# Mamba gate product in four parts beside the sums of its chunk pairs, its square in two, and a fourth tile of merged blocks in the last FFN

## The chip, the cores and the metric

The kernel runs on one core of one Trainium2 chip. Such a core has five engines that run at the same time, each taking its own instructions in their written order: TensorE (PE, matmuls; its weight loads are the row PEld), VectorE (DVE), ScalarE (ACT), GpSimd (POOL), and SyncE (SP), which here only issues DMAs. They meet through semaphores. The metric is the device time of one execution in microseconds (us), the median of several runs. PE reads the on-chip memory SBUF and writes PSUM[...].

## What is computed

The reference has two layers on an image batch of shape (4, 128, 64, 64). Layer 0 is a convolution-and-Mamba hybrid, layer 1 attention and a mixture-of-experts FFN. The change lies in layer 0. Its core is the Mamba block, cut to what matters:

```python
zxbcdt = x @ in_w.T + in_b
z, xBC, dt = ...                       # gate, conv input, step
xBC = _silu(conv3(xBC) + conv_b)       # xs, B, C
y = _ssd(xs * dt[..., None], dt * A, Bm, Cm)   # chunks of 64 tokens, states carried on
y = y + D[None, None, :, None] * xs
y = y.reshape(b, l, di) * _silu(z)             # the gate product
y = y * jax.lax.rsqrt(jnp.mean(y * y, -1, keepdims=True) + 1e-05) * rms_w
return y @ out_w.T
```

One Mamba runs on 8 seed channels made from the 128; two more, one after the other (a cascade), run on each of eight groups of 16 channels. Layer norms follow, and an FFN: a 1x1 convolution to 256 channels, a 3x3 depthwise convolution, GELU, a 1x1 convolution back. Everything is fp32.

## The kernel before, in words

**Items.** A picture has 4096 tokens; they are worked in blocks of 512, eight to a picture. One item is one Mamba on one block: 8 seed items and 4 batches x 8 blocks x 2 cascade levels = 64 cascade items, 72 in all. In a block there are `NU` = 4 pairs of 64-token chunks; `ng` is 2 for cascade items and 1 for seed items, so a tile such as `y` or `zs` holds 1024 or 512 elements in each of 128 partitions.

**Stages of an item.** `outer` loads and normalizes the block. `prep` makes the steps `dt`, their running sums `acs` (a DVE scan) and the decays; on POOL it makes `u` and `cdx`. `front` projects (PE: `ps_z`, `ps_x`, `ps_B`, `ps_C`; ACT: silu into `zs`, `xs`, `Bc`, `Cc`), forms the chunk products (`ps_g`, then `gm` on DVE) and the chunk states (`ps_st`), carries the states on by two DVE scans (`cd<-cd,ps_st`, with `inj` and a small add ahead of them), and multiplies the carried states with C (`ps_yo`, then `y<-ps_yo,y` on DVE). `back` forms the decay matrix (`ps_d`, then its exponentials `e` on ACT, weighed by `gm` on DVE: `e<-e,gm`), multiplies it with the inputs (`within(u)`: 64 matmuls into two PSUM banks, `bank<-e,xp`), and adds the sums to `y` for each chunk pair u: four DVE instructions `y<-bank,const,y`. When all four pairs are added, `back` goes on:

```python
nc.gpsimd.tensor_mul(zs, y, zs)            # L690
yield
yield
nc.scalar.activation(y, zs, AF.Square)     # L693
yield
...
pm = product("ps_ms", self.ms, by_token(y))   # L708
```

Then follow the logarithm and exponential for the root, the matmul `ps_out<-zs`, and the rest of the layer.

**What sets the order.** At a time `back` of one item, `front` of the next, `prep` of the one after and `outer` of a further one are recorded together, and, beside them, the FFN of the batch that was finished last. `Deck` records each instruction with the tiles it reads and writes; `flush` then lets a model of the engines choose the order on each. An instruction's rank is its place in the recording, moved by a table (`BEHIND`); a tile of a ring opens only when the ring has room; and the model never lets a POOL instruction and a DVE instruction with two SBUF inputs run at once (`lockers`, L934). The instructions are then issued in the order chosen, which the chip follows on each engine; so a change of one instruction's size or of its inputs can move others too. All instructions issued this way carry line 1031 in the profile, and are told apart by their tiles.

**FFN of layer 0.** `ffn` (L1348) goes over the eight blocks of a batch: `merge(k)` loads a block (`outs`), takes its layer norm and adds the seed part (`gf`, `ps_det`) and the normalized input (`xg`); `expand(k-1)` makes the 256 channels (`ps_h`, and `ps_hh` for the rows that border on the next block); `conv` does the depthwise taps on DVE (`acc`); `close(k-2)` applies the GELU, multiplies back (`ps_f`), adds on DVE (`t`) and POOL (`t<-t,xin`) and stores. The tiles `outs` have 3 buffers, `xg` (input blocks, used by `merge` and by `close`) 4, `acc` 3. The FFNs of the first three batches run beside the Mamba items; the last one runs when these are done, with four of nine taps on PE (`ps_taps`) and beside the first projections of layer 1 (`tk`, `xl`, `qf`, `kf`, `vf`).

Of the kernel before, what the change touches and what calls it, by code (L numbers as in the profile page):

```python
# [20 lines left out]
F32 = mybir.dt.float32  # L21
F32R = mybir.dt.float32r
U32 = mybir.dt.uint32
AF = mybir.ActivationFunctionType
# [7 lines left out]
LB = 512  # L32
# [243 lines left out]
class Mamba:  # L276
# [344 lines left out]
    def back(self, it, out):  # L621
        sh, s, nc = self.sh, self.s, self.sh.nc
        work, const, ng = sh.work, sh.const, s.ng
        y, zs = it["y"], it["zs"]
        y4 = y.rearrange("p (u g c l) -> p u g c l", u=NU, g=ng, c=2)
        es = {}

        def exponentials(u):
            rt = it["rt"]
            ds = [sh.wide("ps_d") for _ in range(2)]  # L630
            for j2 in range(2):
                for g in range(ng):
                    for j in (2 * j2, 2 * j2 + 1):
                        rows = slice(32 * j, 32 * j + 32)
                        dv = ds[j2][:, j % 2, 0:256 * ng].rearrange("s (h g l) -> s h g l", h=4, g=ng)
                        for c in range(2):
                            nc.tensor.matmul(dv[:, :, g, :], lhsT=sh.lt[rows, g, u, Q * c:Q * c + 128],
                                             rhs=rt[rows, :, u, c, :], start=c == 0, stop=c == 1)
            es[u] = []
            for k in range(2):  # L640
                e = work.tile([128, 4, 2, ng * Q], F32, tag="e", bufs=E_BUFS, name="e")
                nc.scalar.activation(e.rearrange("s h j x -> s j h x"),
                                     ds[k][:, :, 0:256 * ng].rearrange("s j (h x) -> s j h x", h=4), AF.Exp)
                es[u].append(e)

        def weigh(u):
            U, i = divmod(u, 2)
            for k, e in enumerate(es[u]):

                e2 = e.rearrange("s h j x -> s h (j x)")  # L650
                gm = it["gm"][U][:, 2 * i + k].rearrange("s j x -> s (j x)")
                nc.vector.scalar_tensor_tensor(e2, e2, 1.0, gm[:, None, :].to_broadcast([128, 4, 2 * ng * Q]),
                                               ALU.min, ALU.mult)

        def within(u):
            U, i = divmod(u, 2)

            pyv = [t[:, 0:128 * ng].rearrange("p (h x) -> p h x", h=2) for t in sh.psy.tiles("py")]
            for k, e in enumerate(es.pop(u)):
                for g in range(ng):  # L660
                    for f in range(2):
                        for jj in range(2):
                            j = 2 * k + jj
                            for c in range(2):
                                rows = slice(64 * c, 64 * c + 64)
                                nc.tensor.matmul(pyv[c][32 * j:32 * j + 32, :, Q * g:Q * g + Q],
                                                 lhsT=it["xp"][U][rows, g, 4 * i + j, 16 * f:16 * f + 32],
                                                 rhs=e[rows, 2 * f:2 * f + 2, jj, Q * g:Q * g + Q],
                                                 start=f == 0, stop=f == 1)
            for f, name in enumerate(("even", "odd")):  # L670
                for c in range(2):
                    part = pyv[c][:, f, :].rearrange("p (g l) -> p g l", g=ng)
                    nc.vector.scalar_tensor_tensor(y4[:, u, :, c, :], part, const(name), y4[:, u, :, c, :],
                                                   ALU.mult, ALU.add)

        exponentials(0)
        yield
        exponentials(1)
        weigh(0)
        yield  # L680
        for u in range(NU):
            within(u)
            if u + 1 < NU:
                weigh(u + 1)
            if u + 2 < NU:
                exponentials(u + 2)
            yield


        nc.gpsimd.tensor_mul(zs, y, zs)  # L690
        yield
        yield
        nc.scalar.activation(y, zs, AF.Square)  # L693
        yield

        def by_token(t):
            return t.rearrange("p (u g c l) -> p g c u l", u=NU, g=ng, c=2)

        def product(name, lhsT, rhs):

            p, n = sh.ps(name), 128 // ng
            for g in range(ng):
                rows = slice(n * g, n * g + n)
                nc.tensor.matmul(p[rows].rearrange("p (c u l) -> p c u l", c=2, l=Q), lhsT=lhsT[:, g, rows],
                                 rhs=rhs[:, g], start=True, stop=True)
            return p

        pm = product("ps_ms", self.ms, by_token(y))  # L708
        r = y[:, 0:LB]
        nc.scalar.activation(r, pm, AF.Ln, bias=sh.eps, scale=4.0 / s.nh)  # L710
        yield
        nc.scalar.activation(r, r, AF.Exp, scale=-0.5)
        yield
        yield
        out(product("ps_out", self.wo, by_token(zs)), r)
        yield
# [428 lines left out]
def layer0(tc, T, td, const, ident, eps, where, batches, qkv):  # L1145
# [8 lines left out]
    nc = tc.nc  # L1154
    with ExitStack() as ctx:
# [47 lines left out]
        deck = Deck(nc)  # L1203
        nc = sh.nc = deck
# [5 lines left out]
        work = ring(ctx, "work", 2)  # L1210
# [5 lines left out]
        sh.psy = Halves(deck, scan.enter_context(tc.tile_pool(name="psy", bufs=1, space=PSUM)))  # L1216
        gfd = dram.tile([128, L], F32, name="gfd")

        def load(b, k, work=work):
            xin = work.tile([128, LB], F32, tag="xg", bufs=4, name="xin")  # L1220
            nc.sync.dma_start(out=xin, in_=T["x"][b, :, blk(k)])
            return xin

# [124 lines left out]
        def ffn(b, work, ps, depth=0, diag=0, taps=None, ps_taps=None):  # L1348
# [18 lines left out]
            def merge(k):  # L1367

                y = work.tile([128, LB], F32, tag="outs", bufs=3 + depth, name="outs")
                outs[k] = y  # L1370
                nc.sync.dma_start(out=y, in_=td[b, :, blk(k)])
                yield
                yield
                pm = ps("ps_mean")
                nc.tensor.matmul(pm, lhsT=const("avg"), rhs=y, start=True, stop=True)
                nc.vector.scalar_tensor_tensor(y, y, gmix, pm, ALU.add, ALU.subtract)
                yield
                r = work.tile([128, LB], F32, tag="sq", name="ln_r")
                nc.scalar.activation(r, y, AF.Square)
                gf = work.tile([128, LB], F32, tag="ys", name="gf8")[0:8, :]  # L1380
                nc.sync.dma_start(out=gf, in_=gfd[32 * b:32 * b + 8, blk(k)])
                xg = load(b, k, work)
                yield
                pv = ps("ps_var")
                nc.tensor.matmul(pv, lhsT=const("avg"), rhs=r, start=True, stop=True)
                rsqrt(nc, r, pv, eps)
                yield
                nc.vector.tensor_mul(y, y, r)
                normed(b, xg)
                pd = ps("ps_det")  # L1390
                nc.tensor.matmul(pd, lhsT=P("detok", slice(0, 8)), rhs=gf, start=True, stop=True)
                nc.vector.scalar_tensor_tensor(y, y, P("n2w"), pd, ALU.mult, ALU.add)
                nc.vector.scalar_tensor_tensor(y, y, bias2, xg, ALU.add, ALU.add)
                yield
# [38 lines left out]
            def conv(k):  # L1433

                accs[k] = []
                for g in range(2):
                    acc = work.tile([128, LB], F32, tag="acc", bufs=3 + depth, name="acc")
                    sums = made[k].pop(0) if k in made else None
                    for i in range(diag, 9):
                        w = P("dw")[:, 9 * g + i:9 * g + i + 1]  # L1440
                        if sums is None:
                            nc.vector.tensor_scalar(rows(acc), tap(g, i), w, None, ALU.mult)
                        else:
                            nc.vector.scalar_tensor_tensor(rows(acc), tap(g, i), w, sums, ALU.mult, ALU.add)
                        sums = rows(acc)
                        if i % 3 == 2:
                            yield
                    accs[k].append(acc)

            def close(k):  # L1450
# [2 lines left out]
                for g, a in enumerate(acc):  # L1453
                    nc.scalar.activation(a, a, AF.Gelu_apprx_tanh, bias=P("dw_b")[:, g:g + 1])
                nc.scalar.preload_act_table_set(LNEXP)
                xin = load(b, k, work)
                yield
                pf = ps("ps_f")
                for g in range(2):
# [69 lines left out]
        def single(tag, bufs):  # L1529
            return lambda name: pp.tile([128, LB], F32, tag=tag, bufs=bufs, name=name)  # L1530

        pending = deck.staged("ffn", ffn(pending, last, single("f", 4), 0, 4, taps, single("t", 2)))
        run((pending, FFN), (deck.staged("early", early()), 5 * NBLK + 7))
        deck.flush(tc)

# [501 lines left out]
```

## Time and profile before

| | |
|---|---|
| median of 3 runs | 8414.19 us (8400.1 to 8424.57) |
| profiled execution | 8410.01 us |
| its span, first to last instruction | 8408.0 us |
| granted PE clock, mean | 0.948 |
| Mamba items, with the first three FFNs | 60 to 3540 us |
| last item's end, last FFN with first projections | 3540 to about 3763 us |
| attention and experts | from there to the end |

The page of the profile gives busy times of each engine and the costliest groups of instructions. A group is named by line, engine, operation and tiles, written as output<-inputs. The view of waits gives who waited for whom in total; the timeline gives single instructions with their start, length and the idle time ahead of them; stage windows give busy times in stretches of the span. All can be cut to a stretch, an engine or a tile.

### The profile page before, as it was taken

What the parts mean: (1) busy time and instruction counts of PE and PEld (TensorE: products, weight loads), DVE (VectorE), ACT (ScalarE), POOL (GpSimd) and SP (SyncE); (2) the same over time, 40 slices, a digit from 0 to 9 for tenths busy, and PEclk for the clock granted to TensorE, in tenths of its full rate; (3) what the DMA queues carried; (4) which work ended last, traced back from release to release, by engine and by line L of the source; (5) the groups of instructions that cost most, each with busy time, mean ns of one, the idle gap of its engine ahead of it and who ended that gap; (6) DMA issues with size and microseconds to landing.
All of it is one profiled execution on the core that took longest, in us unless ns stands there. A gap on an engine that the chain in (4) does not pass through costs nothing.

```text
span 8408.0 us, 191225 instructions
## 1 busy us (share of the span) xinstructions
PE 7635.6 (91%) x80284; PEld 4548.2 (54%) x80284; DVE 6326.8 (75%) x11211; ACT 5095.5 (61%) x6444; POOL 4737.9 (56%) x3225
## 2 busy tenths in 40 slices
PE   5888888888888888789999999999999999999998
PEld 3566666666666666534554555555555545555554
DVE  6767667887788788767777777777777777777775
ACT  5767677777777777654555555555555555555554
POOL 1111111111111111107999999999999999999997
PEclk8899899988999999889999999999999999999999
DMA  4211111121121112135454545454545545444442
GB/s 143 84 51 45 54 47 50 54 56 50 51 58 52 51 54 57 34 122 132 125 133 125 130 118 138 120 127 128 127 122 132 131 120 131 118 119 119 120 120 60
DMA packets 306604, 800.54 MB, mean 95 GB/s; under 512 B 43984, under 2 KB 61008, under 8 KB 288848
## 3 DMA queue, kind: packets, MB, share of 16 engines
q1 hardware_dynamic: 304848, 780.94, 35.3%
q8 instruction: 633, 10.37, 0.5%
q10 hardware_dynamic: 432, 5.12, 0.2%
q0 software_dynamic: 464, 2.25, 0.1%
q14 instruction: 227, 1.86, 0.1%
HBM read 595.19 MB, written 192.94 MB: 94 GB/s over the span
## 4 chain that ended last, share of the span: by engine, by line
PE 51%; POOL 25%; DVE 10%; ACT 7%; issue 5%; DMA 2%; SPq 0%; POOLq 0%; DVEq 0%; ACTq 0%
POOL s L1885 14%; PE ps_mx L1841 7%; POOL es L1887 6%; PE acc L1900 6%; PE ps_s L1879 5%; PE bank L1031 4%; PE ps_s L1873 3%; PE ps_x L1031 2%; PE ps_B L1031 2%; PE ps_d L1031 2%; DVE y L1031 2%; PE ps_C L1031 2%; PE ps_yo L1031 2%; DVE e L1031 2%; POOL zs L1031 1%
## 5 line engine op out<-in xcount | busy, mean ns | idle before, releaser
L1843 DVE TENSOR_REDUCE mx<-ps_mx 128x1 f32<-128x512 f32 x4096 | 2789.4, 688 | 818.8 <-PE ps_mx L1841 811.4
L1883 ACT ACTIVATE e<-ps_s 128x1024 f32<-128x1024 f32 x2048 | 1985.9, 1022 | 1723.9 <-PE ps_s L1879 1604.5
L1885 POOL TENSOR_TENSOR s<-e 128x1024 f32<-128x1024 f32 x1024 | 2442.8, 2386 | 210.4 <-ACT e L1883 205.0
L1841 PE MATMUL ps_mx<-k,q 128*128 128x512 f32 x4096 | 1879.3, 468 | 57.4 <-DVE mx L1843 23.2
L1887 POOL TENSOR_TENSOR es<-s 128x512 f32<-128x512 f32 x1024 | 1312.1, 1281 | 80.3
L1879 PE MATMUL ps_s<-q,k 128*128 128x512 f32 x4096 | 1281.7, 394 | 0.0
L1900 PE MATMUL acc<-e,V 128*32 128x512 f32 x8192 | 1096.3, 607 | 0.0
L1841 PEld LDWEIGHTS ps_mx<-k,q 128*128 128x128 f32 x4096 | 774.9, 189 | 528.7 <-DVE mx L1843 216.9
L1879 PEld LDWEIGHTS ps_s<-q,k 128*128 128x128 f32 x4096 | 773.3, 189 | 138.6 <-issue 2.7
L1031 DVE SCALAR_TENSOR_TENSOR e<-e,gm 128x1024 f32<-128x1024 f32 (+1 forms) x576 | 663.3, 1162 | 28.8 <-ACT e L1031 27.3
L1873 PEld LDWEIGHTS ps_s<-mr,ones 32*128 32x128 f32 x4096 | 200.4, 181 | 889.9 <-ACT e L1883 414.7
L1031 ACT ACTIVATE e<-ps_d 128x1024 f32<-128x1024 f32 (+1 forms) x576 | 547.0, 974 | 111.3 <-PE ps_d L1031 92.1
L1031 POOL TENSOR_TENSOR u<-acs 128x512 f32<-128x512 f32 x72 | 74.8, 1039 | 926.5 <-DVE acs L1031 907.2
L1031 DVE SCALAR_TENSOR_TENSOR y<-bank,const,y 128x128 f32<-128x128 f32 (+1 forms) x1152 | 365.8, 336 | 266.1 <-PE bank L1031 264.2
L1873 PE MATMUL ps_s<-mr,ones 32*128 32x512 f32 x4096 | 531.5, 496 | 20.3 <-ACT e L1883 20.3
L1031 PE MATMUL bank<-e,xp 64*32 64x128 f32 x17408 | 473.3, 283 | 62.6 <-DVE y L1031 59.1
L1031 PE MATMUL ps_d<-rt,lt 32*128 32x256 f32 x4352 | 422.4, 317 | 52.1 <-ACT y L1031 15.1
L1031 PEld LDWEIGHTS bank<-e,xp 64*32 64x32 f32 x17408 | 373.1, 110 | 145.7 <-DVE y L1031 99.3
L1031 PEld LDWEIGHTS ps_d<-rt,lt 32*128 32x128 f32 x4352 | 306.4, 195 | 222.3 <-ACT e L1031 49.9
L1900 PEld LDWEIGHTS acc<-e,V 128*32 128x32 f32 x8192 | 161.4, 108 | 363.5 <-issue 356.0
L1031 PE MATMUL ps_ms<-y,const 128*64 128x512 f32 (+1 forms) x272 | 133.7, 1033 | 237.7 <-ACT y L1031 233.7
L1031 POOL TENSOR_TENSOR zs<-y,zs 128x1024 f32<-128x1024 f32 (+1 forms) x72 | 173.6, 2411 | 311.1 <-DVE y L1031 311.0
(349 smaller groups left out, 11961.3 us busy)
## 6 DMA issues: line engine op xcount, KB each, us to landing
k<-kd SPq DMA_DIRECT2D x512, 512.0 KB, 7.1
x<-hl SPq DMA_DIRECT2D x256, 256.0 KB, 5.1
V<-vd SPq DMA_DIRECT2D x128, 512.0 KB, 11.4
cd<-raw SPq DMA_DIRECT2D x256, 256.0 KB, 5.2
parts<-cd SPq DMA_DIRECT2D x128, 512.0 KB, 5.6
xin<-in_x SPq DMA_DIRECT2D x128, 256.0 KB, 3.6
q<-qd SPq DMA_DIRECT2D x512, 64.0 KB, 4.5
hl<-hi SPq DMA_DIRECT2D x72, 256.0 KB, 2.0
```

Of the source, the lines that this page charges most:

```text
L1031: getattr(getattr(self.nc, op.engine), name)(*[self.real(a) for a in args], **{k: self.real(a) for k, a in kw.items()})
L1841: nc.tensor.matmul(p, lhsT=q4s[u][:, 128 * qt:128 * qt + 128], rhs=k4s[u][:, blk(kb)], start=True, stop=True)
L1843: nc.vector.tensor_reduce(mxs[u][:, qt, kb:kb + 1], p, AX.X, ALU.max)
L1873: nc.tensor.matmul(pts[j // 2][:, j % 2, :], lhsT=ones2[rows, :], rhs=mrows[u][rows, :], start=True, stop=False)
L1879: nc.tensor.matmul(pts[j // 2][:, j % 2, :], lhsT=k4s[u][:, 128 * kt:128 * kt + 128], rhs=q4s[u], start=False, stop=True)
L1883: nc.scalar.activation(e[:, 2 * j:2 * j + 2], pts[j], AF.Exp)
L1885: nc.gpsimd.tensor_add(s2, e[:, 0:2], e[:, 2:4])
L1887: nc.gpsimd.tensor_add(s, s2[:, 0], s2[:, 1])
L1900: nc.tensor.matmul(accs[u][32 * j:32 * j + 32, :], lhsT=Vs[u][:, 4 * g + j, :], rhs=e[:, j, :], start=g == 0, stop=g == 7)
```

## The change

The gate product is issued in `back`'s loop over the chunk pairs, right after the work of pair u, and only on that quarter of the tile (256 elements for cascade items, 128 for seed items). The square is issued as two ACT instructions, one for each half. In the FFN, the parameter `depth` now adds to the buffers of `outs` and takes from those of `xg`, while `acc` stays at 3; the last FFN is called with depth 1 (4, 3, 3) in place of 0 (3, 4, 3). The other FFNs keep depth 0. The numbers of steps (`yield`) in `back` stay as they were.

```diff
             if u + 2 < NU:
                 exponentials(u + 2)
+
+            part = slice(256 * ng // 2 * u, 256 * ng // 2 * (u + 1))
+            nc.gpsimd.tensor_mul(zs[:, part], y[:, part], zs[:, part])
             yield
 
 
-        nc.gpsimd.tensor_mul(zs, y, zs)
-        yield
-        yield
-        nc.scalar.activation(y, zs, AF.Square)
+        yield
+        yield
+        half = 256 * ng
+        for part in (slice(0, half), slice(half, 2 * half)):
+            nc.scalar.activation(y[:, part], zs[:, part], AF.Square)
         yield
...
-        def load(b, k, work=work):
-            xin = work.tile([128, LB], F32, tag="xg", bufs=4, name="xin")
+        def load(b, k, work=work, bufs=4):
+            xin = work.tile([128, LB], F32, tag="xg", bufs=bufs, name="xin")
...
-                xg = load(b, k, work)
+                xg = load(b, k, work, 4 - depth)
...
-                    acc = work.tile([128, LB], F32, tag="acc", bufs=3 + depth, name="acc")
+                    acc = work.tile([128, LB], F32, tag="acc", bufs=3, name="acc")
...
-                xin = load(b, k, work)
+                xin = load(b, k, work, 4 - depth)
...
-        pending = deck.staged("ffn", ffn(pending, last, single("f", 4), 0, 4, taps, single("t", 2)))
+        pending = deck.staged("ffn", ffn(pending, last, single("f", 4), 1, 4, taps, single("t", 2)))
```

## The prediction

> **What bounds the kernel now.** The page comes first: TensorE (PE) is busy 91% of the span, no other engine over 75%. Cut by stage, the scan stage that the change touches lies at 60 to 3540 us. Columns: busy us of PE, weight loads, DVE, ACT, POOL, with instruction counts; then clock and DMA share.
>
> ```profile
> PE 7635.6 (91%) x80284; PEld 4548.2 (54%) x80284; DVE 6326.8 (75%) x11211; ACT 5095.5 (61%) x6444; POOL 4737.9 (56%) x3225
> 60.00:3540.00 3480.00, 2948.07 (x54190) 2121.41 (x54195) 2638.24 (x4490) 2508.12 (x3336) 447.06 (x537) 0.90 0.20 55
> ```
>
> PE is busy 2948 of 3480 us here, DVE 2638, ACT 2508, POOL 447. What matters is the 532 us that PE idles: the view of waits, cut to PE and this stretch (total us, times, longest).
>
> ```profile
> PE ps_ms L1031 <- ACT y L1031: 227.3, 59, 7.6
> PE bank L1031 <- DVE y L1031: 59.1, 89, 2.4
> PE ps_yo L1031 <- DVE cd L1031: 42.1, 27, 4.0
> ```
>
> One wait is 43% of it: `ps_ms`, the mean square over heads, waits for the square, which waits for the gate product. Now one item in the timeline, item 25 of 72 (start, length, engine; last bracket: idle before).
>
> ```profile
> 1217.87 1.56 PE L1031 MATMUL bank<-e,xp 64*32 64x128 f32 x62 [0.16 <-DVE y L1031]
> 1219.36 2.07 PE L1031 MATMUL ps_st<-xd,bT 64*64 64x32 f32 x128
> 1221.97 0.34 DVE L1031 SCALAR_TENSOR_TENSOR y<-bank,const,y 128x128 f32<-128x128 f32 x1
> 1222.78 2.35 POOL L1031 TENSOR_TENSOR zs<-y,zs 128x1024 f32<-128x1024 f32 x1
> 1225.17 1.06 ACT L1031 ACTIVATE y<-zs 128x1024 f32<-128x1024 f32 x1 [1.59 <-POOL zs L1031]
> 1226.28 1.98 PE L1031 MATMUL ps_ms<-y,const 128*64 128x512 f32 x4 [4.85 <-ACT y L1031]
> 1226.44 1.22 DVE L1031 TENSOR_TENSOR_SCAN cd<-cd,ps_st 128x512 f32<-128x512 f32 x1
> 1229.02 0.65 PE L1031 MATMUL ps_yo<-Cc,last_casc 64*32 64x64 f32 x16
> ```
>
> The last sum `y` ends at 1222.31. Product and square follow (POOL's `u` holds the product back by 0.47), and `ps_ms` starts 3.97 us after `y`, PE having idled 4.85. Over the 63 full cascade items the chain from `y` to `ps_ms` averages 3.92 us: start 0.26, product 2.51, square 1.06, handovers 0.09. But DVE is busy throughout: its second state scan `cd`, which `ps_yo` needs, ends only at 1227.66. That sets how much of the wait can be gained.
>
> [...]
>
> ```profile
> 1479.13 2.81 POOL L1031 TENSOR_TENSOR zs<-y,zs 128x1024 f32<-128x1024 f32 x1
> 1479.66 2.84 DVE L1031 TENSOR_TENSOR sd<-sd,u 128x512 f32<-128x512 f32 x1
> ```
>
> The gate product first waits for DVE's two-input `a`, then runs its 2.35 us while `sd`, 0.68 us when alone, waits for it and takes 2.84. [...]
>
> **The change part by part.**
> *Product.* One POOL instruction becomes four. 1024 elements take 2.35 us and 512 (seed items, shortest) 1.28: a slope of 2.09 ns per element, so 256 take 0.75. The 160-wide `cdx` (0.53 us) lies on the same line. Only the last part follows the last `y`: 2.51 becomes 0.75 on the chain. POOL's total grows from 2.35 to 3.0 us an item, which its 13% load hides.
> *Square.* 1024 elements cost 1.06 us, 512 cost 0.63 (both rows exist). The first half can run early; the chain keeps 0.63. ACT pays 0.2 us more an item, hidden in its 28% idle; without that cover 13 us. The written order holds two more table loads (1.28 us each): 3 us at most.
> *Chain.* 0.3 start + 0.75 + 0.63 + 0.1 = 1.8 us against 3.92: 2.1 us less. Over the items that wait this would be about 125 us.
> *What is late next.* After `ps_ms`, PE needs `ps_yo`, hence the second `cd`. I walked the written order of both kernels over 62 cascade items with durations from the rows. PE's work from the last `bank` to `ps_ms` (mean 3.3 us before, 3.4 after) starts 3.86 us ahead of the last `y`'s end (measured; 3.64 in the changed order, where DVE has 0.22 us less between the pair's sums). `ps_ms` may not start before the chain ends, nor `ps_yo` past its first 16 matmuls before DVE has worked from the last `y` to the second `cd` (5.0 us before, 4.9 after). The walk gives for before 250 us waiting at `ps_ms` and 36 at `ps_yo`, 286 together, against 227 and 42 measured, so it reads about 6% high. For the changed order it gives 116 and 97: 213. The chain gains 134, the scan takes 61 back; net 73 us. In some items the changed order even puts `ps_yo` ahead of `ps_ms`; these gain least.
> *Seed items.* Parts of 128 elements (0.48 us) and half squares (0.41) cut a 2.4 us chain to 1.05, eight times; but the order moves a `ps_g` out of the cover (1.1 us): 5 us net.
> *Port.* Three parts an item now fall between DVE's two-input `e<-e,gm`. If half the parts meet one and hold it 0.35 us, that is 0.5 us of DVE an item, 40% of it reaching PE: 13 us. The last part sometimes meets `inj` or `a`: 0.1 us an item, 6 more. Cost 20. Bounds: -15 (before's own collisions, like the 2.84 above, vanish) to +142 (3 x 0.75 x 63, all on the path).
> *Last FFN.* `outs` gets a fourth buffer, the `xg` ring falls from four to three; `acc` stays three, and the middle FFNs keep their sizes.
>
> ```profile
> 3673.12 0.74 DVE L1031 SCALAR_TENSOR_TENSOR t<-ps_f,pb,outs 128x512 f32<-128x512 f32 x1
> 3673.89 0.32 SPq L1031 DMA_DIRECT2D outs<-td  x1
> 3676.59 1.12 PE L1031 MATMUL ps_mean<-outs,const_sb 128*128 128x512 f32 x2 [0.19 <-DMA outs<-td]
> ```
>
> The load is issued 0.03 us after `t` frees the buffer; with a fourth it need not wait. The `xg` load of a merge now takes the slot that the POOL add of three blocks before freed; that add ended a block ago, so SP, where the load stands ahead of the projections' stores, does not stop there. From 3590 to 3763 us PE idles 20 us, about 10 of it in this chain (waits of `ps_var` 6.8, `ps_mean` 1.6, `ps_h` 1.5). Bounds 0 to -10; I take -6.
> *Sum.* -73 - 5 + 20 - 6 = -64, against the profiled execution's own 8410 us (span 8408): 8346. The runs' median is 4 us higher, so 8350. Attention, from 3763 on, is untouched.
>
> **Rivals.**
> *The whole wait is gained.* DVE idles 24% of the scan, so its queue might follow PE forward. Against: item 25, where DVE never rests from `y` to `cd`. 125 + 5 + 6 less 10 for the port is 126: about 8288.
> *Everything is given back.* DVE's work between `y` and `cd` differs in the rewritten order from item to item (1.4 to 7.6 us); if `ps_yo` loses 1 us an item more than walked, 62 us go and the gain with them: about 8412.
> *Slower[...].* The early parts lie beside `e<-e,gm`, which feeds `bank`, PE's largest work. If every part stops DVE for its 0.75 us on that path, 142 us are lost against 84 gained: 8414 + 58 = 8472. It decides against the change when DVE loses over 1.3 us an item on the path. For it: `e` stands right behind the pair's sums in many items. Against: [...] 24% idle time.
>
> **How the numbers follow.** Half given back: 0.50, own range 8315 to 8387. Whole wait: 0.16, 8250 to 8315. Given back: 0.16, within 0.3% (25 us, about what a measurement here can tell). Slower: 0.18, 8439 to 8480, its middle near 8450, since not every part will stop DVE fully. Faster is the first two, 0.66. The range for eight in ten drops the far halves of the whole-wait and the slower case (0.17): 8280 to 8450.
>
> **What would show it.** Right: `zs` four times an item near 0.75 us; squares 0.63; `ps_ms <- ACT y` falls from 227 to near 120 while `ps_yo <- DVE cd` rises from 42 to near 95; the scan stage some 60 us shorter. Wrong: `ps_yo` unchanged (whole gain), or `e<-e,gm` well over its 1222 ns mean and more `bank` wait (port), or new waits elsewhere from the rewritten order, which the walk doesn't see beyond `ps_yo`; `outs` loads still issued right behind `t`.

## The result, and the profile after

The changed kernel takes 8399.12 us (median of 19 runs, 8375.46 to 8422.16) against 8414.19 (19 runs, 8400.1 to 8433.43): a ratio of 0.998, with a 95% interval of 0.9971 to 0.999. That is 15 us, a small gain, and less than the 25 us that the prediction called about what a measurement here can tell. The forecast was 8350. The time lies in its range, 8280 to 8450, but in the case that it called given back (chance 0.16), not in the likeliest one. One run of the study, of e2 below, took 10815 us at a mean clock of 0.606, far from all others, and is left out of e2's numbers.

The profiled execution took 8403.3 us against 8410.01. First the stage view of the kernel after, for the stretch of the scan (busy us of PE, weight loads, DVE, ACT, POOL; then the granted clock, DMA share and GB/s):

```profile
60.00:3540.00 3480.00, 2995.92 (x53841) 2143.47 (x53842) 2608.38 (x4471) 2504.73 (x3394) 607.60 (x748) 0.89 0.20 55
```

PE is busy 48 us longer than before in this stretch and has done less in it: 53,841 matmuls against 54,190. Now the view of waits for PE of the kernel after, in the same stretch (total us, times, longest):

```profile
PE ps_ms L1035 <- ACT y L1035: 115.7, 49, 4.8
PE ps_yo L1035 <- DVE cd L1035: 84.4, 49, 3.0
PE bank L1035 <- DVE y L1035: 35.3, 48, 2.1
...
PE ps_g L1035 <- DVE gm L1035: 30.5, 24, 2.4
```

The two waits that the forecast worked out came as told: 227.3 became 115.7 (forecast 116) and 42.1 became 84.4 (forecast 97), together 69 us less. And yet the last of the 72 items reaches its `ps_ms` at 3570.3 us, against 3551.9 before: the scan got 18 us *longer*. Up to that point PE idled 496 us in place of 538, which is 42 less; but it was busy 3015 us in place of 2954, 61 more, with the same 54,296 matmul records. The groups of instructions say how that can be. Kernel before, then after (last part: busy us, mean ns of one):

```profile
L1031 PE MATMUL ps_out<-zs,wc_casc 128*64 128x512 f32 x252 | 79.6, 715 | 0.4
L1031 PE MATMUL ps_ms<-y,const 128*64 128x512 f32 x252 | 118.7, 1040 | 216.1 <-ACT y L1031 216.1
```

```profile
L1035 PE MATMUL ps_out<-zs,wc_casc 128*64 128x512 f32 x252 | 102.9, 908 | 1.3 <-ACT ln_r L1035 0.5 <-ACT y L1035 0.4
L1035 PE MATMUL ps_ms<-y,const 128*64 128x512 f32 x252 | 108.0, 951 | 104.3 <-ACT y L1035 101.8 <-DVE cd L1035 2.6
```

The same 252 matmuls of `ps_out`, of the same shape, went from 715 to 908 ns: more of them ran at half clock. One item shows it, item 14 (counted from 0) in PE's timeline (start, length; last bracket: idle before). Before:

```profile
706.60 1.97 PE L1031 MATMUL ps_ms<-y,const 128*64 128x512 f32 x4 [4.05 <-ACT y L1031]
708.51 0.90 PE L1031 MATMUL ps_cd<-cdx,const 128*128 128x160 f32 x2
...
712.83 0.74 PE L1031 MATMUL ps_d<-rt,lt 32*128 32x256 f32 x8
713.50 1.08 PE L1031 MATMUL ps_out<-zs,wc_casc 128*64 128x512 f32 x4
```

After:

```profile
702.32 1.16 PE L1035 MATMUL ps_g<-Cc,Bc 64*64 64x64 f32 x64 [1.73 <-DVE gm L1035]
...
709.77 0.72 PE L1035 MATMUL ps_yo<-Cc,cd 64*32 64x64 f32 x32 [1.54 <-DVE cd L1035]
712.87 2.36 PE L1035 MATMUL ps_yo<-Cc,cd 64*32 64x64 f32 x80 [2.37 <-DVE cd L1035]
715.16 1.22 PE L1035 MATMUL ps_d<-rt,lt 32*128 32x256 f32 x8
716.31 1.98 PE L1035 MATMUL ps_ms<-y,const 128*64 128x512 f32 x4
...
720.20 1.98 PE L1035 MATMUL ps_out<-zs,wc_casc 128*64 128x512 f32 x4
```

Before there is one long wait, and the half clock that begins in it (705.87 to 712.69 us) is over after some 6 us of work: `ps_d` runs in 0.74 us and `ps_out` in 1.08. After, the written order has `ps_yo` ahead of `ps_ms`. There are three shorter waits (1.73, 1.54, 2.37), and the wait for the square is quite gone; but `ps_d` takes 1.22 and `ps_out` 1.98, as `ps_ms` does. The stage view of the kernel after gives the clock of these stretches (columns as above):

```profile
690.00:711.30 21.30, 16.38 (x540) 13.41 (x536) 17.51 (x30) 13.31 (x20) 6.27 (x6) 0.92 0.03 7
711.30:724.90 13.60, 12.03 (x115) 7.38 (x116) 7.17 (x9) 5.88 (x8) 2.13 (x2) 0.50 0.01 2
```

For 13.6 us the clock stood at half, with 12 us of work in it.

The trace records the granted clock over time; laid over PE's busy stretches it splits them into work at full and at half clock. The table does this from 60 us to the last item's first `ps_ms`. "Full-clock work" is busy time less half of the time at half clock, an estimate from these two of what the same work would take at full clock.

| kernel | last `ps_ms` at | PE idle | PE busy | of it at half clock | full-clock work |
|---|---|---|---|---|---|
| before | 3551.9 | 538 | 2954 | 554 | 2676 |
| after | 3570.3 | 496 | 3015 | 688 | 2671 |

The work is the same to 0.2%; in these two profiles the busy time differs because 134 us more of it ran at half. Half of that is 67 us, which covers the 61.

But a profile is a single run. The mean granted clock is on record for every run. The clock is 1.0 or 0.5 throughout the traces of before and after; where that holds, the missing share of the mean, doubled, times the span, is the time at half clock. The mean is 0.9448 over the 19 runs of after, and 0.9459 to 0.9473 over the sets of runs of before that the experiments were set against. The profiled run of before, at 0.948, lies above these means, that of after, at 0.944, below its own. By the means the change has some 15 to 40 us more time at half clock in the whole kernel, where the two profiles are 77 us apart. So the profiles show the direction and overstate the size.

### The profile page after: what moved, and what is told of

Same layout as the page of the kernel before. It is cut to its first block, busy times and chain, and to the rows that moved or that the text cites. A ratio compares the mean times of both kernels' runs of the same rounds, so it can differ in the third digit from the quotient of the medians.

```text
span 8401.5 us, 191443 instructions
## 1 busy us (share of the span) xinstructions
PE 7681.8 (91%) x80284; PEld 4579.0 (55%) x80284; DVE 6315.2 (75%) x11211; ACT 5105.5 (61%) x6518; POOL 4902.6 (58%) x3441
## 4 chain that ended last, share of the span: by engine, by line
PE 30%; POOL 21%; issue 3%; DVE 2%; ACT 1%; DMA 0%; SPq 0%; POOLq 0%; DVEq 0%; ACTq 0%
POOL s L1889 13%; PE ps_mx L1845 7%; PE acc L1904 6%; POOL es L1891 6%; PE ps_s L1883 6%; PE ps_s L1877 3%; PE ps_e L1793 2%; PE ps_den L1917 1%; DVE mx L1847 1%; PE ps_taps L1035 1%; PE ps_sh L1864 0%; POOL parts L1707 0%; PE ps_f L1782 0%; POOL cx L1709 0%; PE ps_f L1781 0%
## 5 line engine op out<-in xcount | busy, mean ns | idle before, releaser
L1035 POOL TENSOR_TENSOR zs<-y,zs 128x256 f32<-128x256 f32 (+1 forms) x288 | 314.1, 1091 | 1256.3 <-DVE y L1035 1255.6
L1800 DVE SCALAR_TENSOR_TENSOR acc<-ps_e,w,acc 128x128 f32<-128x128 f32 x896 | 312.5, 349 | 47.6 <-PE ps_e L1793 15.2
L1035 DVE SCALAR_TENSOR_TENSOR acc<-h,pb,acc 128x512 f32<-128x512 f32 x448 | 338.1, 770 | 7.8
```

The source lines that it names most:

```text
L1035: getattr(getattr(self.nc, op.engine), name)(*[self.real(a) for a in args], **{k: self.real(a) for k, a in kw.items()})
L1800: nc.vector.scalar_tensor_tensor(acc, pe[:, 128 * j:128 * j + 128], we, acc, ALU.mult, ALU.add)
```

## The experiments

Theory of the clock: the edit trades one long wait for more, shorter ones, and PE's clock stands at half for longer. Theory of the order: the edit is good, but the order that `Deck` newly plans for it costs as much as it gains. Theory of the port, by the prediction's name for it: the parts hold up VectorE, as the product did `sd` there (2.84 us, 0.68 when alone). What is behind this no run shows. The part in the last FFN is taken off first. Times are set against runs of the kernel before on the same chip; ratios are given with their 95% intervals.

**The last FFN alone (e1).** The kernel before with the FFN hunks of the diff only:

```diff
-            xin = work.tile([128, LB], F32, tag="xg", bufs=4, name="xin")
+            xin = work.tile([128, LB], F32, tag="xg", bufs=bufs, name="xin")
...
-        pending = deck.staged("ffn", ffn(pending, last, single("f", 4), 0, 4, taps, single("t", 2)))
+        pending = deck.staged("ffn", ffn(pending, last, single("f", 4), 1, 4, taps, single("t", 2)))
```

> The kernel before with the last FFN's part of the change alone (a fourth tile of merged blocks); the scan is untouched. The prediction had priced this part at -6 us. The two traces instead show the stretch from the last square's sum to the first sum of the attention going from 236.9 to 214.9 us. If that belongs to the FFN's part, this kernel takes 8392 us, 22 us less than before, with the scan's last sum at the same place (3552 us) as before. If it is the scan's changed end that gave it, the gain is near 6 us or below.

Measured: 8404.42 us, ratio 0.999 (0.9979 to 1.0): 13 us less, in an interval that reaches 1.0. From the last `ps_ms` to the first sum of the attention (`ps_mx`) its profile has 224.3 us against 236.9, also 13 less. So the FFN's part gives about 13 us, between the 22 and the 6 of the expectation. The waits of PE in the last FFN, 3597 to 3757 us of this run:

```profile
PE ps_mean L1031 <- DVE kf L1031: 9.1, 5, 2.0
PE ps_q L1031 <- ACT v L1031: 4.0, 1, 4.0
```

The waits on the chain of `outs` (`ps_var`, `ps_h`, and `ps_mean` for the load; 6.8, 1.5 and 1.6 us before) are gone; others grew, `ps_mean` for `kf` from 4.6 us and `ps_q` from 0.2.

**The scan's part alone (e2).** The changed kernel with the last line of the diff undone:

```diff
-        pending = deck.staged("ffn", ffn(pending, last, single("f", 4), 1, 4, taps, single("t", 2)))
+        pending = deck.staged("ffn", ffn(pending, last, single("f", 4), 0, 4, taps, single("t", 2)))
```

> The scan's part of the change alone (product in four, square in two); the last FFN as before. Every theory that adds the two parts up expects what e1 leaves: if e1 gains 22 us, this one is 5 to 18 us slower than before (8419 to 8432), with the scan's last sum near 3570 us against 3552, TensorE's idle time in the scan some 36 us lower and its busy time some 60 us higher. If e1 gains only 6 us, this one gains 9.

Measured: 8409.35 us (median of 13 runs), ratio 0.9989 (0.9977 to 1.0): 8 us less, nearer to the second case of the expectation than to the first. With e1's 13 us the two parts add up to some 20 us, the change's 15 to within what can be measured. In this kernel's profile the last `ps_ms` stands at 3575.4, PE idles 500 and is busy 3015 us, 685 of it at half clock. So the scan's part by itself is worth nothing that can be told from zero.

**The split in the old order (e3).** The planner sees the whole product and the whole square, and plans the order of before; the parts are issued as soon as the sums of their pair are:

```diff
+            for extra in list(self.extras):          # in flush, behind each issued op
+                extra[0].discard(id(op))
+                if not extra[0]:
+                    self.extras.remove(extra)
+                    for engine, name, args in extra[1]:
+                        getattr(getattr(self.nc, engine), name)(*[self.real(a) for a in args])
...
         nc.gpsimd.tensor_mul(zs, y, zs)
+        nc.ops[-1].calls = [("tensor_mul", (zs[:, part[3]], y[:, part[3]], zs[:, part[3]]), {})]
+        for u in range(3):
+            nc.extras.append((pair_done[u], [("gpsimd", "tensor_mul", (zs[:, part[u]], y[:, part[u]], zs[:, part[u]]))]
+                              + [("scalar", "activation", (y[:, half[0]], zs[:, half[0]], AF.Square))] * (u == 2)))
...
         nc.scalar.activation(y, zs, AF.Square)
+        nc.ops[-1].calls = [("activation", (y[:, half[1]], zs[:, half[1]], AF.Square), {})]
```

> The kernel before with its written order kept on every engine: parts 0 to 2 of the product are issued right behind the sums of their pair, the fourth part and the second half of the square stand where the whole ones stood, the first half right behind part 2. The last FFN as before. Theory of the clock (shorter and more frequent waits leave TensorE's granted clock at half for longer): the waits ahead of the sum fall as in the change, by 90 to 110 us, but TensorE's busy time in the scan rises by 30 to 60 us from 2954, and the time is 8340 to 8400. Theory of the order (the newly planned order of the scan costs the time, the split gains it): the walk over the old order with the parts in it gives 100 us less than before, busy time rises by at most 15 us, and the time is 8310 to 8340. Theory[...] (the parts hold up VectorE): no gain, 8400 to 8440, with VectorE's instructions beside the parts longer.

**The new order without the split (e4).** The order of e2 on PE and DVE, row for row, but the product and the square are issued whole:

```diff
             nc.gpsimd.tensor_mul(zs[:, part], y[:, part], zs[:, part])
+            nc.ops[-1].calls = [("tensor_mul", (zs, y, zs), {})] if u == NU - 1 else []
...
             nc.scalar.activation(y[:, part], zs[:, part], AF.Square)
+            nc.ops[-1].calls = [("activation", (y, zs, AF.Square), {})] if part.start else []
```

> The changed scan's planned order, but the product and the square whole, at the places of the fourth part and of the second half; parts 0 to 2 and the first half aren't issued. The last FFN as before. The walk over this order gives 288 us of waits against 286 of before. Theory of the clock: the waits are long ones again, TensorE's busy time in the scan is near the 2954 us of before, and the time is 8400 to 8440. Theory of the order: the cost of the order stands alone without the gain of the split, 8470 to 8520, and TensorE's busy time is near that of after (3015) although the product is whole.

Measured: e3 8361.82 us, ratio 0.9939 (0.9927 to 0.9952), 55 us less; e4 8531.27 us, ratio 1.0133 (1.0119 to 1.0148), 114 us more. PE's waits in the scan, e3 first, then e4:

```profile
PE ps_ms L1041 <- ACT y L1041: 136.7, 61, 5.7
PE bank L1041 <- DVE y L1041: 79.4, 97, 2.4
PE ps_yo L1041 <- DVE cd L1041: 51.7, 38, 2.5
```

```profile
PE ps_ms L1037 <- ACT y L1037: 214.0, 51, 6.6
PE ps_yo L1037 <- DVE cd L1037: 96.7, 44, 4.0
```

| kernel | last `ps_ms` at | PE idle | PE busy | at half clock | full-clock work |
|---|---|---|---|---|---|
| e2, split, new order | 3575.4 | 500 | 3015 | 685 | 2672 |
| e3, split, old order | 3503.6 | 479 | 2964 | 574 | 2678 |
| e4, whole, new order | 3686.4 | 605 | 3022 | 706 | 2669 |

This decides between the theories, though not by e3's time, which lies in the range of the theory of the clock (8340 to 8400). The split does not bring the half clock: in the old order PE's busy time rises by 10 us only, against before, where that theory had 30 to 60. The new order brings it, split or not: 685 and 706 us in the profiles. The mean clocks of all runs say so more firmly: 0.9466 for before, 0.9510 for e3, 0.9458 for e2 and 0.9392 for e4, which is 899, 819, 912 and 1036 us at half clock in the whole kernel. The split in the old order takes 80 us of half clock off; the new order puts 93 us on with the split, and 137 without it. The theory of the order also told the sign and about the size of e4 (8470 to 8520; 8531), where the theory of the clock had 8400 to 8440. Its value for e3, 8310 to 8340, was 22 us too low. The two waits fell by 81 us there and not by 100, and `bank <- DVE y` rose by 20. With that goes a longer `e<-e,gm`: 1286 ns on average, 64 more than before.

In numbers: the new order costs 114 us with the whole product, and 48 with the split (e2 against e3); the split gives 55 us in the old order and about 120 in the new one.

**Both parts in the old order (e5).** e3 with the FFN hunks of e1.

> The split product and square in the written order of before (as in e3), with the last FFN's part of the change on top (as in e1). If the two add up, -55 us and -13 us give 8414 - 68 = 8346 us, the scan's last sum at 3504 us and the first sum of the attention some 223 us after it. If they share a gain (the end of the scan hides the FFN's loads anyway), 8355 to 8365.

Measured: 8355.19 us against 8424.12, ratio 0.9915 (0.9901 to 0.9928): 69 us less, so the two add up. (The 8346 us expected were set against 8414, a lower time of before than the one measured beside this run.) A caution comes with it. Its profile has the same order in the scan as e3, yet the last `ps_ms` at 3528.3 and 644 us at half clock, where e3 had 3503.6 and 574. Single profiles of one order thus differ by 25 us here, and a gap of that size between two profiles says nothing. The 18 us between before and after above are such a gap; e2, e3 and e4 rest on their medians and mean clocks.

**Keeping the clock up (e6, e7).** Matmuls of constants are put where PE would wait: n of them ahead of `ps_ms`, into its own bank, and m ahead of `ps_yo`. What they write is overwritten.

```diff
-            for name, args, kw in op.calls:
+            for name, args, kw in op.ahead + op.calls:
...
         pm = product("ps_ms", self.ms, by_token(y))
+        warm = dict(lhsT=const("avg"), rhs=const("reset"), start=True, stop=True)
+        nc.ops[-1].ahead = [("matmul", (pm,), warm)] * n
...
+        nc.ops[-1].ahead = [("matmul", (d[:, 0:LB],), warm)] * m
```

e6 is the changed kernel with n = 3 and m = 2, e7 is e5 with 2 and 2.

> The changed kernel with constant matmuls of no use to the result, issued where TensorE would wait: three into ps_ms's own bank ahead of ps_ms, two into the first bank of ps_yo ahead of ps_yo[...]. Theory of the clock: the waits are filled, the half clock after them goes, TensorE's own work at half clock falls from 688 us to below 550, and since the work of the scan waits on TensorE the scan shortens by 30 to 60 us: 8340 to 8375. Rival: the queues of VectorE and ScalarE set the end of each item, a faster TensorE only waits longer: within 12 us of after, 8385 to 8415. A third end: the fillers cost more than the clock gives, in the items that don't wait: 8420 to 8450.

> The kernel of e5 with two constant matmuls ahead of ps_ms and two ahead of ps_yo. Theory of the clock: of its 575 us at half clock 100 or more go, 20 to 40 us below e5. Rival (VectorE and ScalarE set the end): within 12 us of e5. Fillers too dear: 15 to 40 us above e5.

Measured: e6 8401.22 us, ratio 0.9974 (0.9966 to 0.9982), which can't be told from after's 0.998; it lies in the range of the rival, for which the other engines set the end. e7 8336.83 us, 0.9895 (0.9879 to 0.991), 18 us below e5, just under the 20 to 40 expected. In both the work at half clock fell to less than half: 276 us in e6, 303 in e7. But a filler was priced wrongly. It takes two passes of 0.5 us at full clock, 1.0 us (two fillers took 1.98 us in e9's timeline below), four times the author's estimate: e6 has 360 fillers, and 345 us more full-clock work than after. So it may be that the clock gave nothing here, or that five fillers in every item ate what it gave; e11 tells these apart.

**A third order (e8).** The scan's part alone, but in the planner's model the parts may run beside DVE's two-input instructions:

```diff
-                            e == "gpsimd" and lockers["vector"] > now + 1e-9):
+                            e == "gpsimd" and not op.part and lockers["vector"] > now + 1e-9):
...
-                if op.both or e == "gpsimd":
+                if (op.both or e == "gpsimd") and not op.part:
                     lockers[e] = end
```

> The scan's part of the change alone (FFN as before), but the model that plans the written order lets the four parts run beside VectorE's two-input instructions[...]. That gives a third written order: 1006 lines of TensorE's order differ from before, against 1301 in the planned order of the change, and 1229 from that one. If the loss comes from the parts' lock in the model, which pushes VectorE's instructions aside there, this order loses less than the change's: 8340 to 8390. If any newly planned order loses, because the table of ranks fits the old recording, it is near e2's 8411: 8395 to 8450.

Measured: 8408.08 us against 8424.12, ratio 0.998 (0.9974 to 0.9987). Quite another order, about the same loss: 0.4 points, some 35 us, against e3's 0.9939. The parts' lock in the model is not what makes the new order bad. Nor is the clock in this one: its mean over the 21 runs is 0.9504, which is 0.0045 above before's on this chip, and e3's was 0.0044 above. Here `ps_yo` hardly waits:

```profile
PE ps_ms L1038 <- ACT y L1038: 149.4, 64, 4.7
...
PE ps_yo L1038 <- DVE cd L1038: 13.1, 10, 2.3
```

The two waits sum to 162 us, fewer than e3's 188, and still the last `ps_ms` stands at 3574.7, with 510 us idle and 625 at half clock (this profiled run lies 19 us above its median, as e5's lies 9 above). What costs the time in this order is open.

**Fewer fillers, and fillers alone (e9, e10, e11).** e9 is e7 with 2 and 1 fillers; e10 is the kernel before with 3 and 1; e11 is the changed kernel with 1 and 1.

> The kernel of e7 with one constant matmul ahead of ps_yo in place of two (two ahead of ps_ms as there). A filler took 0.5 us at full clock in e7's trace ([...]some 0.94 us for a pair of matmuls), and the wait at ps_yo was 1.2 us where there was one. If the second filler there is mostly beyond the wait, this gains 5 to 20 us on e7: ratio to before 0.987 to 0.989. If the half clock returns without it (from 303 us of work at half clock to over 400), it loses 5 to 15: 0.990 to 0.9915.

> The kernel before with three constant matmuls ahead of ps_ms and one ahead of ps_yo, nothing else changed. It tells what the clock alone is worth where the chain from the last sum of y to ps_ms is whole. Theory of the clock: 554 us of work at half clock fall below 330, some 100 us less of TensorE time, but ps_ms can't start before the square is done, so only what follows the wait gains: 15 to 50 us faster, 8370 to 8405 against 8420. Rival (the other engines set every item's end): within 12 us of before.

> The changed kernel with one constant matmul ahead of ps_ms and one ahead of ps_yo (e6 had three and two). In e6 the work at half clock fell from 688 to 276 us and the fillers cost 342 us of full-clock work, more than the waits that they replaced. With 144 fillers the cost is some 140 us. If the fillers that fall into no wait ate e6's gain, this one is 10 to 30 us below after: ratio 0.9945 to 0.997. If the clock isn't what holds the changed order up, it stays within 8 us of after: 0.997 to 0.999.

Measured, against 8410.06 us: e9 8300.81, ratio 0.988 (0.9865 to 0.9895); e10 8357.45, 0.994 (0.9926 to 0.9953); e11 8357.0, 0.994 (0.9926 to 0.9953). e10 shows that the clock is worth something by itself: with the chain from `y` to `ps_ms` untouched, useless matmuls make the kernel before 53 us faster, net of what they cost, at a mean clock of 0.973 against 0.947; that is a little more than the 15 to 50 expected. e11, a little faster than expected too, shows that e6's fillers had eaten their own gain: with two in an item the changed kernel is 0.4 points below itself. e9 came as expected, though its expectation still had a filler at half of what it takes. For e9, item 14 again, in PE's timeline:

```profile
694.14 1.98 PE L1046 MATMUL ps_ms<-const,const_sb 128*128 128x512 f32 x4
696.06 1.08 PE L1046 MATMUL ps_ms<-y,const 128*64 128x512 f32 x4
697.07 0.54 PE L1046 MATMUL ps_cd<-cdx,const 128*128 128x160 f32 x2
697.44 1.02 PE L1046 MATMUL ps_yo<-const,const_sb 128*128 128x512 f32 x2
...
700.85 0.74 PE L1046 MATMUL ps_d<-rt,lt 32*128 32x256 f32 x8
701.52 1.08 PE L1046 MATMUL ps_out<-zs,wc_casc 128*64 128x512 f32 x4
```

The fillers (`ps_ms<-const`, `ps_yo<-const`) stand where the waits were, and everything behind them runs at full clock: `ps_ms` 1.08 us in place of 1.97, `ps_cd` 0.54 in place of 0.90. e9 is the fastest kernel of the study, 1.2% below before.

**The order with equal fillers (e12).** e5 with 1 and 1 fillers; it differs from e11 in the written order only.

> The old written order with the split and the last FFN's part (e5), and one constant matmul ahead of ps_ms and one ahead of ps_yo, just as many as in e11. It differs from e11 in the written order alone. In e3 and e2, without fillers, the two orders lay 0.5 points of the ratio apart. If the new order loses only through the clock, the gap shrinks with the half clock, to 0.3 points or less: 0.991 to 0.994. If the order also costs by new waits of other places, some of the gap of 0.5 to 0.7 stays: 0.986 to 0.990.

Measured: 8325.95 us against 8411.92, ratio 0.989 (0.9871 to 0.9908), against e11's 0.994 (0.9926 to 0.9953). The gap is 0.5 points by these ratios and 0.4 by the medians, some 33 us: of the two cases, the second. The work at half clock is nearly alike in the two profiles (408 and 432 us), but over all runs the mean clocks are 0.9655 in e12 and 0.9622 in e11, which is 58 us of half clock. Half of these, 29 us, is the most that the clock can be of the 33. So e12 alone does not show that the new order costs more than the clock; e8 shows it of its own order. The profiles don't settle it: e11's profiled run lies 12 us below its median and e12's 8 above, and their scans are only 11 us apart.

## Why the prediction went wrong

*Product, square, chain: right.* After, from the profile of the scan:

```profile
L1035 POOL TENSOR_TENSOR zs<-y,zs 128x256 f32<-128x256 f32 x252 | 284.9, 1131 | 1150.9 <-DVE y L1035 1150.3
L1035 ACT ACTIVATE y<-zs 128x512 f32<-128x512 f32 x126 | 79.2, 628 | 126.3 <-POOL zs L1035 126.2
L1035 DVE SCALAR_TENSOR_TENSOR e<-e,gm 128x1024 f32<-128x1024 f32 x504 | 614.6, 1232 | 22.5 <-ACT e L1035 21.3
```

The square takes 628 ns, as forecast. From the last `y` to `ps_ms` it now takes 1.97 us on average (forecast 1.8, before 3.92). A part of the product takes 1131 ns and not 750: of the 256 parts of cascade items, the 67 that overlap an `e<-e,gm` take 1.76 us on average, the others 0.92. The last part of an item takes 0.96.

*What is late next: right for these two waits.* 69 us net against 73, with each of the two near its number. At the place that the forecast named, the second `cd`, 42 us were taken back.

*Port: the hold-up is there, but was priced too dear.* 20 us were set, the author's estimate. In the changed order `e<-e,gm` went from 1222 to 1232 ns, 5 us in all, and the wait of `bank` fell. In the old order (e3) it is 64 ns and 33 us of DVE, and `bank` waits 20 us more. The parts that overlap an `e<-e,gm` take 0.84 us longer than the others (1.76 against 0.92), so in the changed order it is mostly POOL's part that is held up. The slower rival falls.

*Seed items: wrong sign.* Item 8, the first behind the seed items, has its `ps_ms` at 425.8 us, against 422.2 before. In the old order (e3) it is 417.9: the forecast 5 us were to be had only there, as far as single profiles tell.

*The sum: here it failed.* The step that failed is the price of the rewritten order. Apart from `ps_yo`, where the walk ended, the sum put it at nothing, and it took every matmul's duration as fixed. "New waits elsewhere from the rewritten order" stood only among what would make it wrong, with no price and no case of its own. The runs show in its place that, with the same split, the new order takes 48 us more than the old one (e2, e3), about the 49 us by which result and forecast differ. The two waits that had a price are little of this: they sum to 200 us in the profile of after and to 188 in e3's.

In the profiles of before and after this has two parts. PE's idle time fell by 42 us and not by 69; `ps_g` for `gm` alone rose from this line of before to 30.5 us:

```profile
PE ps_g L1031 <- DVE gm L1031: 7.2, 15, 0.7
```

And the sum subtracted waits, but added nothing for the 61 us by which the same matmuls became longer. For the scan, -69 + 27 + 61 = +19, where the two `ps_ms` marks say +18; the forecast had -58. The page of before had the clue: a granted clock of 0.90 in this stretch.

How much of the 48 us is the clock is known as a bound only. By the mean clocks the new order has 93 us more at half clock, and half of that, 46 us, is the most that it can cost. Between the 41 runs of before that stand beside e5 to e8, each us more at half clock goes with 0.32 us more time; by that rate, an estimate, the 93 us are some 30 of the 48. In e8 a new order costs some 35 us at e3's clock. So the clock is one path by which an order costs, and not the only one; the others stay open.

*Last FFN: too small.* -6 was taken and 13 measured (e1), beyond the bound of 10. The stretch from the last `ps_ms` to the attention took 236.9 us before, 234.4 in e2 and 233.9 in e3; with the fourth buffer it took 224.3 in e1, 219.4 in e5, and 215.0 in the changed kernel, 22 less than before. The stage view of the last FFN, before and then after:

```profile
3590.00:3763.00 173.00, 152.84 (x404) 68.89 (x402) 129.53 (x188) 102.93 (x169) 11.10 (x9) 0.94 0.34 111
```

```profile
3605.00:3757.00 152.00, 137.25 (x392) 64.68 (x391) 131.56 (x188) 104.71 (x169) 11.49 (x9) 1.00 0.39 125
```

The term that was priced is about right: from the last `ps_ms` on PE idles 60 us before, 52 in e1 and 48 after. Busy time makes up the rest, and it had no term: 177 us before, 172 in e1, 167 after. In e1 the work at half clock is nearly as before (38 and 36 us), in the changed kernel it is 25; so some 6 of the 22 us are clock again, with the other sign, in single profiles. The 4 us by which PE's work at full clock is lower in both were not explained.

*The rivals.* "Everything is given back" has the right time (8412) and the wrong mechanism: it wanted `ps_yo` to lose 62 us more than walked, and `ps_yo` lost less. That the time fell near its number is luck. What gave the gain back was the order, partly through the clock. Which placement in the new order is the costly one was not settled; e8 shows only that a second newly planned order loses as well.

## What to carry to other kernels

Where a planner writes the order, an edit is two changes: the edit, and a new order everywhere. Run each without the other before judging either; here the split alone gave -55 us, the new order alone +114, and both together 8 us less. And when the limiting engine's granted clock is lower with its waits than with them filled, as here (0.947 in the mean before, 0.973 in e10), idle time taken out is not time gained: price the work behind each wait at the clock that the new waits will leave, and look at the mean duration of one unchanged matmul group before and after. Take the mean clock over many runs for it: two profiles of one order (e3, e5) differed by 70 us of work at half clock. Work that the kernel has no use for can pay for itself where it stands in a wait (53 us net in e10).

## What the runs showed of the hardware

The granted clock takes two values in the traces of before and after, 1.0 and 0.5, and in the scan it stands at half for multiples of 3.41 us. A single wait of that length is not needed for it: in the changed kernel 95 of the 110 half-clock stretches of the scan began with no gap of PE as long as 3.41 us reaching into the 3.41 us ahead; in 80 the largest was under 2.5 us. Before, 55 of 99 began with no gap of that length.

The stretches can be cut into windows of 3.41 us. In the changed kernel PE idled for over a fifth of 54 of these windows, and after none of them did full clock come back; before, after none of 61. So, in these two traces, idle time of over some 0.7 us in all within such a window always went with another one at half. A busy window is not enough either: of the 134 in the changed kernel with PE busy for 99% or more, 91 were followed by full clock and 43 were not. Item 14 above is an example: PE works without a gap from 712.87 us on, and full clock comes back at 724.94. What else decides is not shown. Long stretches are more frequent in the new order: 29 of the 110 lasted three windows or more, against 20 of 99 before and 18 of 108 in e3.

Matmuls of constants ahead of two waits, about 1.0 us each at full clock, were worth 0.4% of the whole kernel with one and one (e11) and 0.6% with three and one (e10), with nothing else changed.
